# Two cross attentions in one kernel: every row block of x turned by VectorE into the moving blocks of the query products, without a DRAM copy, and in another order

## The chip, the cores and the metric

The kernel runs on one core of a Trainium2 chip. The metric is the time of one execution in microseconds, as the device reports it; the median of the runs shown is taken. All data are float32.

## What is computed

x is 4 sequences of 1024 tokens by 1024 features (4096 rows), the context 4 times 64 rows of 1024 features. Two cross attentions follow each other, and each attends from the rows of x to the 64 context rows of its own sequence:

```
# layer 0: 32 query heads of 32 features, 8 key/value heads, additive mask
q = x @ Wq + bq ; k = ctx @ Wk + bk ; v = ctx @ Wv + bv
p = softmax(q k^T / sqrt(32) + mask0)
x1 = layernorm((p v) @ Wo + bo + x) * gamma + beta
# layer 1: 16 heads of 64 features, boolean mask over the context, gated residual
a = layernorm(ctx) ; Q = x1 @ Wq1.T ; K = a @ Wk1.T ; V = a @ Wv1.T
p = softmax(where(mask1, Q K^T * 64**-0.5, -inf))
y = x1 + tanh(gate) * (p V) @ Wo1.T
```

## The kernel before, in words

**Stages.** The program has four stages. (1) Keys and values of both layers are computed from the context (to about 82 us in the profile). (2) The queries of layer 0 are computed in four blocks of 1024 tokens, numbered 0 to 3; beside block b + 1's products runs the attention of block b, one subtile of 128 tokens after the other (32 subtiles; to about 640 us). (3) Beside the attention of block 3 the key side of layer 1's query weight is folded (`folded_queries`, L729); I call this the fold stage (to about 757 us). (4) Out-projection, normalisation and layer 1 in pairs of subtiles (`project`, L394). Stage 4's code is not touched.

**A query block.** The product of the weight with a block of 1024 tokens is split in two by two blocks of 512 and done with seven products instead of eight, a Strassen-Winograd form. The stationary blocks of the weight (A11, A12, A22 and the sums S1 to S4, `left_weight`, L150) are made once. The moving blocks are made for each query block: B11, B21, B12 and B22 are quarters of the turned rows (feature half, token half), and four sums on VectorE (`right_sums`, L167 to L172) give T1 = B12 - B11 (in B12's buffer), T2 = B22 - T1, T3 = T2 - B11 and N4 = B21 - T2. So seven moving blocks are alive: B11, B21, T1, B22, T3, T2, N4. They share one pool of seven buffers (`wpool`, tag `wb`), and the next block's B11 takes the buffer of the old B11, and so on: a new moving block can be written only when the last product that reads the old one is done.

**Products.** `query_steps` (L537) lists 28 steps for a block: for i = 0 to 3 the products p1, p6, p7, p5, p3, p4, p2, each of four matmuls of 128x128 by 128x512 (L543). p1, p6, p5 and p3 add up in one bank X, p7 and p4 in V, p2 alone in W. After p1, p6, p5 and p3 ScalarE copies X out with the bias (`keep`, L551: e, z, u, f); VectorE adds (`add`, L557) V to u after p5 and to z after p4, and W to e after p2. Each finished tile is stored to `qTd` in DRAM by SP's queue (`put`, L554). Products and their operands: p1 A11 B11, p2 A12 B21, p3 S4 B22, p4 A22 N4, p5 S1 T1, p6 S2 T2, p7 S3 T3.

**Turning rows.** 256 rows ("pair") of x come in as one tile xq (`pair_rows`, four transfers of 256 KB). `turn_quarters` (L367, L370) is a 32x32 block transpose on VectorE, 128x1024 elements an instruction, two for each pair. In blocks 0 and 1 the turns write the moving blocks directly (`fill` in `rows0`, L489). In blocks 2 and 3, `store_turned` (L528) turns the rows during block 0's products into a staging tile (`stpool`) and stores it to `xTd` in DRAM; `load` (L499) brings the quarters back later as transfers of 1 MB. Rows are loaded in the order block 0, blocks 2 and 3, block 1. The moving blocks of block b + 1 are filled in block b's list of steps, after step 21 (B11), 24 (B12), 25 (B22 and three sums) and 27 (B21 and N4).

**Attention of layer 0.** `mix` (L656) does one subtile t: `front` loads q (L600) and makes the scores (matmul L611 into `big`, a pool with one buffer; VectorE L616 adds the mask), then the row maximum (L447), the subtraction (L455), the exponential on ScalarE (L456), the row sum (L465, with a reciprocal) and the division (L470). For subtile t - 1, `flip` turns the probabilities on TensorE (L640) and copies them out on ScalarE (L641), and `values` multiplies by v (L646). Between these pieces `mix` places three or four steps of the next query block, or in the fold stage the steps of `folded_queries` (matmuls L743, evictions L750).

**Order.** Each engine executes its instructions in order. The order on an engine is set when the program is built: a scheduler starts from the program order, and moves instructions where pools and dependencies let it. SP's queue carries nearly all transfers, also in order: an issue that waits for its data holds back those behind it.

Of the kernel before, what the change touches and what calls it, by code (L numbers as in the profile page):

```python
# [66 lines left out]
def tile_two_cross_attentions(  # L67
# [47 lines left out]

    x1 = [dram.tile([2 * P, H], F32, tag=f"x1_{t}", name=f"x1_{t}") for t in range(NPAIR)]
    p1 = [dram.tile([2 * P, H], F32, tag=f"p1_{t}", name=f"p1_{t}") for t in range(NPAIR)]
    xTd = {t: dram.tile([P, KC, TB], F32, tag=f"xT_{t}", name=f"xTd_{t}") for t in range(2, NBLK)}
    oTd = [dram.tile([P, KC, 2 * P], F32, tag=f"oT_{t}", name=f"oTd_{t}") for t in range(NPAIR)]
    qTd = [dram.tile([P, KC, TB], F32, tag=f"qT_{t}", name=f"qTd_{t}") for t in range(NBLK)]  # L120
    v0d = dram.tile([B * S, 256], F32, tag="v0d", name="v0d")
# [5 lines left out]
    def open_pool(stack, name, bufs, side="left"):  # L127
        return stack.enter_context(tc.tile_pool(name=name, bufs=bufs, side=side, reuse_waits="tile"))
# [3 lines left out]
    def new_block(tag, name):  # L132
        return wpool.tile([P, HK, HW], F32, tag=tag, name=name)
# [16 lines left out]
    def left_weight(w, tag, name):  # L150

        r = {"A11": block_of(w, 0, 0, tag, f"{name}_A11", True)}
        r["S2"] = new_block(tag, f"{name}_S2")
        r["S3"] = block_of(w, 0, 1, tag, f"{name}_A21", True)
        r["S1"] = new_block(tag, f"{name}_S1")
        r["S4"] = new_block(tag, f"{name}_S4")
        r["A22"] = block_of(w, 1, 1, tag, f"{name}_A22", True)
        r["A12"] = block_of(w, 1, 0, tag, f"{name}_A12", True)
        tt = nc.vector.tensor_tensor
        return r, [  # L160
            lambda: tt(r["S1"], r["S3"], r["A22"], ALU.add),
            lambda: tt(r["S3"], r["A11"], r["S3"], ALU.subtract),
            lambda: tt(r["S2"], r["S1"], r["A11"], ALU.subtract),
            lambda: tt(r["S4"], r["A12"], r["S2"], ALU.subtract),
        ]
# [21 lines left out]
    def run(steps):  # L187
        for s in steps:
            s()
# [1 line left out]

    attention = ExitStack()
    kv0pool = open_pool(attention, "kv0", 1, "right")
    rows_cm = ExitStack()
    xpool = open_pool(rows_cm, "xrows", 4, "right")
    stpool = open_pool(rows_cm, "xturned", 3, "right")
    scratch_cm = ExitStack()
    scratch = open_pool(scratch_cm, "scratch", 1)

# [6 lines left out]
    for w, n in ((wk0, "wk0"), (wv0, "wv0")):  # L206
        t = wpool.tile([P, KC, 256], F32, tag="wb", name=n)
        nc.sync.dma_start(out=t, in_=w.rearrange("(k p) o -> p k o", p=P))
        wkv0.append(t)
    def constant(ap, shape, name, dt=F32, pool=const):  # L210
        t = pool.tile(shape, dt, tag=name, name=name)
        nc.sync.dma_start(out=t, in_=ap)
        return t
# [16 lines left out]
        for a in range(NQ):  # L230
            queue.dma_start(out=t[a * Q : (a + 1) * Q], in_=v[a])

    def pair_rows(blk, i):
        xq = xpool.tile([P, 2 * NQ, QW], F32, tag="x", name=f"xq{blk}_{i}")
        at = blk * TB + i * 2 * P
        load_quarters(xq, x[at : at + 2 * P, :])
        return xq

    later = [(blk, i) for blk in xTd for i in range(4)]
    order = [(0, i) for i in range(4)] + later + [(1, i) for i in range(4)]  # L240
    ahead = []

    def more_rows():
        if order:
            ahead.append(pair_rows(*order.pop(0)))

    for _ in range(4):
        more_rows()

    ident = const.tile([P, P], F32, tag="ident", name="ident")  # L250
    make_identity(nc, ident)
# [77 lines left out]
    for e in range(2):  # L329
        for i in range(2):  # L330
            j = 2 * i + e
            for c in range(2):
# [3 lines left out]
                    in_=v0d[:, at : at + 32].rearrange("(b s) d -> s b d", b=B),  # L336
                )
    ct = transpose_ctx(1)
    for w, dst, n in ((w1k, kTd, "k1"), (w1v, vTd, "v1")):
        kvT = stpool.tile([P, KC, B * S], F32, tag="st", name=n)  # L340
        for c in range(KC):
            ps = one() if c % 2 else wx()
            for k in range(KC):
                nc.tensor.matmul(
                    ps[:, 0:256], w[k // HK, c // HK][:, k % HK, sub_ap(c % HK)], ct[:, k, :],
                    start=(k == 0), stop=(k == KC - 1),
                )
            nc.scalar.copy(kvT[:, c, :], ps[:, 0:256])
        nc.sync.dma_start(out=dst, in_=kvT)
    tanh_gate = const.tile([P, 1], F32, tag="tanh", name="tanh_gate")  # L350
    nc.scalar.activation(tanh_gate, gate_sb, AF.Tanh)
    run(w_q_sums)
# [131 lines left out]


    queries_cm = ExitStack()
    etmp = open_pool(queries_cm, "etmp", 2)

    def rows0(blk):  # L489

        r = {
            n: new_block("wb", f"x{n}_{blk}") for n in ("B11", "B21", "T1", "B22", "T3", "T2", "N4")
        }

        taken = []

        def load(n):
            h, u = {"B11": (0, 0), "T1": (0, 1), "B22": (1, 1), "B21": (1, 0)}[n]
            nc.sync.dma_start(  # L499
                out=r[n], in_=xTd[blk][:, h * HK : (h + 1) * HK, u * HT : (u + 1) * HT]  # L500
            )

        def fill(n):
            h, u = {"B11": (0, 0), "T1": (0, 1), "B22": (1, 1), "B21": (1, 0)}[n]
            for i in range(2):
                if len(taken) <= 2 * u + i:
                    taken.append(ahead.pop(0))
                turn_quarters(
                    taken[2 * u + i], r[n][:, :, i * 2 * P : (i + 1) * 2 * P],
                    (h * HK, (h + 1) * HK),  # L510
                )
                if h:
                    more_rows()

        f = load if blk in xTd else fill
        sums = right_sums(r)

        def b22():
            f("B22")
            run(sums[:3])  # L520

        def b21():
            f("B21")
            sums[3]()

        return r, {21: lambda: f("B11"), 24: lambda: f("T1"), 25: b22, 27: b21}

    def store_turned(blk, i):  # L528

        xq = ahead.pop(0)  # L530
        st = stpool.tile([P, KC, 2 * P], F32, tag="st", name=f"st{blk}_{i}")
        for h in range(2):
            turn_quarters(xq, st[:, h * HK : (h + 1) * HK, :], (h * HK, (h + 1) * HK))
        more_rows()
        nc.sync.dma_start(out=xTd[blk][:, :, i * 2 * P : (i + 1) * 2 * P], in_=st)

    def query_steps(blk, rows):  # L537

# [50 lines left out]
            keep("f", tmp["X"], i, 0)  # L589
            put("f", i, 0, 1)  # L590

        return [lambda i=i, p=p: p(i) for i in range(HK) for p in (p1, p6, p7, p5, p3, p4, p2)]

    probs = {}

# [88 lines left out]

    rows, fills = rows0(0)
    run(fills.values())
    steps = query_steps(0, rows)
    rows, fills = rows0(1)
    for n, step in enumerate(steps):
        step()  # L690
        if n % 5 in (0, 3) and later:
            store_turned(*later.pop(0))
        if n in fills:
            fills[n]()
    rows_cm.close()

    qpool = open_pool(attention, "q0", 2, "right")
    spool = open_pool(attention, "scores", 4, "right")
    ppool = open_pool(attention, "probsT", 3, "right")
# [29 lines left out]
    def folded_queries(kT, wch, k):  # L729
# [7 lines left out]
        def heads(cc):  # L737
# [8 lines left out]
                    )  # L746
            at = st[cc // 2].rearrange("p b (c e s) -> p c e b s", e=2, s=S)
            for e in range(2):
                for c2 in range(2):
                    nc.scalar.activation(  # L750
                        at[:, (cc % 2) * 2 + c2, e],
                        banks[e][:, c2 * 256 : (c2 + 1) * 256].rearrange("p (b s) -> p b s", b=B),
                        AF.Copy, scale=SCALE1,
                    )
            if cc % 2:
                n = cc // 2
                nc.sync.dma_start(
# [314 lines left out]
```

## Time and profile before

| what | value |
| --- | --- |
| three runs, us | 1986.14, 1985.75, 1980.96 |
| median, us | 1985.75 |
| the profiled execution's own time, us | 1985.84 |
| its span, us | 1983.9 |
| mean granted clock of TensorE | 0.993 of full speed |
| TensorE busy, us of the span | 1930.2 |
| VectorE busy, us of the span | 1275.6 |
| ScalarE busy, us of the span | 352.7 |
| DMA, MB moved | 317.95 |

The profile is one execution. Its engines are called PE (TensorE matmuls), PEld (TensorE weight loads), DVE (VectorE), ACT (ScalarE), POOL (GpSimd) and SP (SyncE); busy times are sums over the span, and an L number is a line of the kernel. A mark such as "<-DVE xT L172" names what ended a wait; "x8" at the end of a timeline row counts matmuls and weight loads joined in that row. PEclk is the clock that the chip granted TensorE, with 1.00 for full speed. "The slices" are the span cut in 40 equal parts, about 49.6 us each, with the busy tenths of each engine.

### The profile page before, as it was taken

The numbers are of one execution on the slowest core, as the hardware profiler recorded it, in microseconds if no ns is written. First come the engines' busy times: TensorE is split into PE (matmuls) and PEld (weight loads), VectorE is DVE, ScalarE is ACT, GpSimd is POOL, SyncE is SP. The second block draws the span as 40 slices with busy tenths as digits, with TensorE's granted clock in tenths as the row PEclk, the third lists the DMA queues.
The fourth block names the chain that finished last, engine by engine and source line by source line (L and its number), as shares of the span: only waits on it lengthen the run. The fifth ranks groups of instructions, "written<-read, shape, count | busy, mean of one in ns | idle before, by whom it ended". The sixth has DMA issues, their size and how long they took to land.

```text
span 1983.9 us, 16593 instructions
## 1 busy us (share of the span) xinstructions
PE 1930.2 (97%) x6208; PEld 921.1 (46%) x6208; DVE 1275.6 (64%) x1540; ACT 352.7 (18%) x628; POOL 236.9 (12%) x103
## 2 busy tenths in 40 slices
PE   8998999999999789999999999999999999999999
PEld 7643454554555554444443444444444444444443
DVE  3534877777777794535557667657675766576653
ACT  1101333333334684122100000000000000000000
POOL 0000000000000001445545543000000000000000
PEclk9999999999999999999999999999999999999999
DMA  8998234334335979376574335446655574647421
GB/s 279 207 245 260 66 98 156 92 98 155 93 98 180 301 255 317 118 231 203 181 223 148 116 106 138 138 124 166 165 139 147 150 180 117 168 129 180 117 85 43
DMA packets 217104, 317.95 MB, mean 160 GB/s; under 512 B 19392, under 2 KB 142656, under 8 KB 214464
## 3 DMA queue, kind: packets, MB, share of 16 engines
q1 hardware_dynamic: 197760, 287.53, 50.5%
q10 hardware_dynamic: 19264, 29.37, 5.5%
q8 instruction: 49, 0.80, 0.2%
q14 instruction: 31, 0.25, 0.0%
HBM read 190.76 MB, written 126.09 MB: 160 GB/s over the span
## 4 chain that ended last, share of the span: by engine, by line
PE 86%; DVE 7%; DMA 4%; ACT 1%; issue 1%; SPq 0%; DVEq 0%; ACTq 0%
PE wx L394 58%; PE wx L543 17%; PE big L611 3%; PE one L646 2%; PE one L640 2%; PE one L772 1%; DVE mx L447 1%; DMA xq<-in_x_dram 1%; DMA wq_A<-in_wq_dram 1%; DVE s L616 1%; DMA q<-qTd 1%; DVE s L455 1%; PE big L772 1%; DVE sm L465 1%; ACT a L750 1%
## 5 line engine op out<-in xcount | busy, mean ns | idle before, releaser
L402 DVE TENSOR_TENSOR r<-wx,r 128x512 f32<-128x512 f32 x224 | 153.7, 686 | 271.2 <-PE wx L394 267.4
L456 ACT ACTIVATE s<-s 128x1024 f32<-128x1024 f32 x96 | 101.3, 1056 | 701.0 <-DVE s L455 692.5
L797 POOL TENSOR_TENSOR r<-r,bo 128x1024 f32<-128x1024 f32 x32 | 78.1, 2448 | 840.0 <-DMA r<-in_x_dram 827.5
L465 DVE TENSOR_REDUCE sm<-s 128x16 f32<-128x1024 f32 x96 | 115.4, 1212 | 34.7 <-ACT s L456 34.7
L543 PE MATMUL wx<-xT,wq_S 128*128 128x512 f32 x256 | 123.6, 625 | 11.5 <-DVE xT L172 10.7
L406 DVE TENSOR_TENSOR s<-wx,key_bias 128x512 f32<-128x512 f32 x64 | 44.1, 689 | 137.3 <-PE wx L394 134.5
L455 DVE TENSOR_TENSOR s<-s,mx 128x1024 f32<-128x1024 f32 x96 | 118.1, 1230 | 1.4
L394 PE MATMUL wx<-wo_B,S 128*128 128x512 f32 x256 | 117.0, 599 | 0.7 <-DVE r L402 0.7
L543 PE MATMUL wx<-xB,wq_A 128*128 128x512 f32 x256 | 116.4, 597 | 0.0
L447 DVE TENSOR_REDUCE mx<-s 128x16 f32<-128x1024 f32 x96 | 115.5, 1204 | 1.3
L394 PE MATMUL wx<-b_B,pT 128*128 128x512 f32 x256 | 116.1, 593 | 0.0
L394 PE MATMUL wx<-b_B,S_p 128*128 128x512 f32 x256 | 116.0, 596 | 0.0
L616 DVE SCALAR_TENSOR_TENSOR s<-big,m 128x1024 f32<-128x1024 f32 x64 | 78.0, 1218 | 59.0 <-PE big L611 59.0
L394 PE MATMUL wx<-a_B,xT 128*128 128x512 f32 x256 | 115.4, 592 | 0.0
L394 PE MATMUL wx<-a_B,S_x 128*128 128x512 f32 x256 | 115.3, 593 | 0.0
L394 PE MATMUL wx<-wo_B,o 128*128 128x512 f32 x256 | 113.8, 595 | 0.0
L470 DVE TENSOR_TENSOR s<-s,sm 128x1024 f32<-128x1024 f32 x92 | 111.4, 1220 | 1.2
L838 POOL TENSOR_TENSOR r<-r,gamma 128x1024 f32<-128x1024 f32 x32 | 76.1, 2377 | 137.3 <-DVE r L275 137.3
L611 PEld LDWEIGHTS big<-kv,q 64*128 64x128 f32 x1024 | 67.4, 187 | 49.0 <-issue 30.6
L611 PE MATMUL big<-kv,q 64*128 64x128 f32 x1024 | 80.7, 285 | 7.0 <-DVE s L616 3.8
L839 POOL TENSOR_TENSOR r<-r,beta 128x1024 f32<-128x1024 f32 x32 | 81.0, 2531 | 2.4
L543 PEld LDWEIGHTS wx<-xT,wq_S 128*128 128x128 f32 x256 | 47.8, 196 | 67.9 <-issue 61.4
(153 smaller groups left out, 2709.8 us busy)
## 6 DMA issues: line engine op xcount, KB each, us to landing
xq<-in_x_dram SPq DMA_DIRECT2D x64, 256.0 KB, 10.0
q<-qTd SPq DMA_DIRECT2D x32, 512.0 KB, 4.7
oTd<-oT SPq DMA_DIRECT2D x32, 512.0 KB, 3.5
ad<-a SPq DMA_DIRECT2D x16, 1024.0 KB, 5.6
o<-oTd SPq DMA_DIRECT2D x16, 1024.0 KB, 8.9
r<-in_x_dram SPq DMA_DIRECT2D x32, 512.0 KB, 4.4
bd<-b SPq DMA_DIRECT2D x32, 512.0 KB, 6.5
x<-r SPq DMA_DIRECT2D x32, 512.0 KB, 2.9
```

What stands on the lines that cost most here:

```text
L394: nc.tensor.matmul(bank, a[s][:, k, :], w[m][:, k, :], start=first and k == 0, stop=last and k == HK - 1, skip_group_check=True,)
L402: nc.vector.tensor_tensor(at, bank, at, ALU.add)
L447: r = nc.vector.tensor_reduce(mx, s, AX.X, ALU.max)
L455: nc.vector.tensor_tensor(s, s, mx.unsqueeze(2).to_broadcast([P, 16, S]), ALU.subtract)
L456: nc.scalar.activation(s, s, AF.Exp)
L465: nc.vector.tensor_reduce(sm, s, AX.X, ALU.add)
L470: nc.vector.tensor_tensor(s, s, sm.unsqueeze(2).to_broadcast([P, 16, S]), ALU.mult)
L543: nc.tensor.matmul(bank, w_q[a][:, k, sub_ap(i)], rows[b][:, k, :], start=first and k == 0, stop=last and k == HK - 1, skip_group_check=True,)
L611: nc.tensor.matmul(ps[:, at : at + P], q[on, c * 4 + g, :], k0bd[on, b, c, :], start=True, stop=True,)
L616: nc.vector.scalar_tensor_tensor(s, ps.rearrange("p (h s) -> p h s", h=16), SCALE0, m.unsqueeze(1).to_broadcast([P, 16, S]), ALU.mult, ALU ...
L797: nc.gpsimd.tensor_tensor(ru, ru, bo_sb, ALU.add)
L839: nc.gpsimd.tensor_tensor(r[u], r[u], beta0_sb, ALU.add)
```

## The change

1. Staging goes: `xTd`, `stpool`, `store_turned` and `load` are removed. All rows come in in the order of the blocks. Blocks 0 and 1 have a pool of four row tiles (`xrows_0`), blocks 2 and 3 one of two (`xrows_1`); `more_rows` issues loads while buffers are free, and `done_with_rows` frees one after its turns.
2. The moving blocks of all four blocks are filled by turns directly, in another grouping: after step 22 B11 and B21 of the first two pairs, after 25 B12 and T1, after 26 B22 and the other three sums.
3. The products of each i run in the order p1, p2, p6, p7, p5, p3, p4.
4. In the fold stage each pair of evictions of 128x256 becomes one of 128x512.
5. `left_weight` loads A12 as the second block instead of the last; the keys and values of layer 1 have a pool of their own, and are stored after block 0's moving blocks are filled.

```diff
     x1 = [dram.tile([2 * P, H], F32, tag=f"x1_{t}", name=f"x1_{t}") for t in range(NPAIR)]
     p1 = [dram.tile([2 * P, H], F32, tag=f"p1_{t}", name=f"p1_{t}") for t in range(NPAIR)]
-    xTd = {t: dram.tile([P, KC, TB], F32, tag=f"xT_{t}", name=f"xTd_{t}") for t in range(2, NBLK)}
     oTd = [dram.tile([P, KC, 2 * P], F32, tag=f"oT_{t}", name=f"oTd_{t}") for t in range(NPAIR)]
     qTd = [dram.tile([P, KC, TB], F32, tag=f"qT_{t}", name=f"qTd_{t}") for t in range(NBLK)]
     v0d = dram.tile([B * S, 256], F32, tag="v0d", name="v0d")
...
     def left_weight(w, tag, name):
         r = {"A11": block_of(w, 0, 0, tag, f"{name}_A11", True)}
+        r["A12"] = block_of(w, 1, 0, tag, f"{name}_A12", True)
         r["S2"] = new_block(tag, f"{name}_S2")
         r["S3"] = block_of(w, 0, 1, tag, f"{name}_A21", True)
         r["S1"] = new_block(tag, f"{name}_S1")
         r["S4"] = new_block(tag, f"{name}_S4")
         r["A22"] = block_of(w, 1, 1, tag, f"{name}_A22", True)
-        r["A12"] = block_of(w, 1, 0, tag, f"{name}_A12", True)
         tt = nc.vector.tensor_tensor
         return r, [
             lambda: tt(r["S1"], r["S3"], r["A22"], ALU.add),
...
     attention = ExitStack()
     kv0pool = open_pool(attention, "kv0", 1, "right")
-    rows_cm = ExitStack()
-    xpool = open_pool(rows_cm, "xrows", 4, "right")
-    stpool = open_pool(rows_cm, "xturned", 3, "right")
+    early_cm = ExitStack()
+    xpools = [open_pool(early_cm, "xrows_0", 4, "right")]
+    kv1_cm = ExitStack()
+    kv1pool = open_pool(kv1_cm, "kv1", 2, "right")
     scratch_cm = ExitStack()
     scratch = open_pool(scratch_cm, "scratch", 1)
...
         t = wpool.tile([P, KC, 256], F32, tag="wb", name=n)
         nc.sync.dma_start(out=t, in_=w.rearrange("(k p) o -> p k o", p=P))
         wkv0.append(t)
     def constant(ap, shape, name, dt=F32, pool=const):
         t = pool.tile(shape, dt, tag=name, name=name)
         nc.sync.dma_start(out=t, in_=ap)
...
         for a in range(NQ):
             queue.dma_start(out=t[a * Q : (a + 1) * Q], in_=v[a])
-    def pair_rows(blk, i):
-        xq = xpool.tile([P, 2 * NQ, QW], F32, tag="x", name=f"xq{blk}_{i}")
-        at = blk * TB + i * 2 * P
-        load_quarters(xq, x[at : at + 2 * P, :])
-        return xq
-    later = [(blk, i) for blk in xTd for i in range(4)]
-    order = [(0, i) for i in range(4)] + later + [(1, i) for i in range(4)]
+    order = [(blk, i) for blk in range(NBLK) for i in range(4)]
     ahead = []
+    free = [4, 2]
     def more_rows():
-        if order:
-            ahead.append(pair_rows(*order.pop(0)))
-    for _ in range(4):
-        more_rows()
+        while order and free[order[0][0] > 1]:
+            blk, i = order.pop(0)
+            free[blk > 1] -= 1
+            xq = xpools[blk > 1].tile([P, 2 * NQ, QW], F32, tag="x", name=f"xq{blk}_{i}")
+            at = blk * TB + i * 2 * P
+            load_quarters(xq, x[at : at + 2 * P, :])
+            ahead.append(xq)
+    def done_with_rows(blk):
+        free[blk > 1] += 1
+        if len(xpools) > 1 or order[0][0] < 2:
+            more_rows()
+    more_rows()
     ident = const.tile([P, P], F32, tag="ident", name="ident")
     make_identity(nc, ident)
...
                     in_=v0d[:, at : at + 32].rearrange("(b s) d -> s b d", b=B),
                 )
     ct = transpose_ctx(1)
+    kv1 = []
     for w, dst, n in ((w1k, kTd, "k1"), (w1v, vTd, "v1")):
-        kvT = stpool.tile([P, KC, B * S], F32, tag="st", name=n)
+        kvT = kv1pool.tile([P, KC, B * S], F32, tag="k1", name=n)
         for c in range(KC):
             ps = one() if c % 2 else wx()
             for k in range(KC):
...
                     start=(k == 0), stop=(k == KC - 1),
                 )
             nc.scalar.copy(kvT[:, c, :], ps[:, 0:256])
-        nc.sync.dma_start(out=dst, in_=kvT)
+        kv1.append((dst, kvT))
     tanh_gate = const.tile([P, 1], F32, tag="tanh", name="tanh_gate")
     nc.scalar.activation(tanh_gate, gate_sb, AF.Tanh)
     run(w_q_sums)
...
     queries_cm = ExitStack()
+    xpools.append(open_pool(queries_cm, "xrows_1", 2))
     etmp = open_pool(queries_cm, "etmp", 2)
     def rows0(blk):
...
             n: new_block("wb", f"x{n}_{blk}") for n in ("B11", "B21", "T1", "B22", "T3", "T2", "N4")
         }
+        sums = right_sums(r)
         taken = []
-        def load(n):
-            h, u = {"B11": (0, 0), "T1": (0, 1), "B22": (1, 1), "B21": (1, 0)}[n]
-            nc.sync.dma_start(
-                out=r[n], in_=xTd[blk][:, h * HK : (h + 1) * HK, u * HT : (u + 1) * HT]
-            )
-        def fill(n):
-            h, u = {"B11": (0, 0), "T1": (0, 1), "B22": (1, 1), "B21": (1, 0)}[n]
+        def turn_into(name, xq, i, h):
+            at = slice(i % 2 * 2 * P, (i % 2 + 1) * 2 * P)
+            turn_quarters(xq, r[name][:, :, at], (h * HK, (h + 1) * HK))
+        def first_half():
             for i in range(2):
-                if len(taken) <= 2 * u + i:
-                    taken.append(ahead.pop(0))
-                turn_quarters(
-                    taken[2 * u + i], r[n][:, :, i * 2 * P : (i + 1) * 2 * P],
-                    (h * HK, (h + 1) * HK),
-                )
-                if h:
-                    more_rows()
-        f = load if blk in xTd else fill
-        sums = right_sums(r)
+                xq = ahead.pop(0)
+                turn_into("B11", xq, i, 0)
+                turn_into("B21", xq, i, 1)
+                done_with_rows(blk)
+        def b12():
+            for i in range(2, 4):
+                taken.append(ahead.pop(0))
+                turn_into("T1", taken[-1], i, 0)
+            sums[0]()
         def b22():
-            f("B22")
-            run(sums[:3])
-        def b21():
-            f("B21")
-            sums[3]()
-        return r, {21: lambda: f("B11"), 24: lambda: f("T1"), 25: b22, 27: b21}
-    def store_turned(blk, i):
-        xq = ahead.pop(0)
-        st = stpool.tile([P, KC, 2 * P], F32, tag="st", name=f"st{blk}_{i}")
-        for h in range(2):
-            turn_quarters(xq, st[:, h * HK : (h + 1) * HK, :], (h * HK, (h + 1) * HK))
-        more_rows()
-        nc.sync.dma_start(out=xTd[blk][:, :, i * 2 * P : (i + 1) * 2 * P], in_=st)
+            for i in range(2, 4):
+                turn_into("B22", taken.pop(0), i, 1)
+                done_with_rows(blk)
+            run(sums[1:])
+        return r, {22: first_half, 25: b12, 26: b22}
     def query_steps(blk, rows):
...
             keep("f", tmp["X"], i, 0)
             put("f", i, 0, 1)
-        return [lambda i=i, p=p: p(i) for i in range(HK) for p in (p1, p6, p7, p5, p3, p4, p2)]
+        return [lambda i=i, p=p: p(i) for i in range(HK) for p in (p1, p2, p6, p7, p5, p3, p4)]
     probs = {}
...
     rows, fills = rows0(0)
     run(fills.values())
+    for dst, kvT in kv1:
+        nc.sync.dma_start(out=dst, in_=kvT)
+    kv1_cm.close()
     steps = query_steps(0, rows)
     rows, fills = rows0(1)
     for n, step in enumerate(steps):
         step()
-        if n % 5 in (0, 3) and later:
-            store_turned(*later.pop(0))
         if n in fills:
             fills[n]()
-    rows_cm.close()
+    early_cm.close()
     qpool = open_pool(attention, "q0", 2, "right")
     spool = open_pool(attention, "scores", 4, "right")
     ppool = open_pool(attention, "probsT", 3, "right")
...
                     )
             at = st[cc // 2].rearrange("p b (c e s) -> p c e b s", e=2, s=S)
             for e in range(2):
-                for c2 in range(2):
-                    nc.scalar.activation(
-                        at[:, (cc % 2) * 2 + c2, e],
-                        banks[e][:, c2 * 256 : (c2 + 1) * 256].rearrange("p (b s) -> p b s", b=B),
-                        AF.Copy, scale=SCALE1,
-                    )
+                nc.scalar.activation(
+                    at[:, (cc % 2) * 2 : (cc % 2) * 2 + 2, e],
+                    banks[e].rearrange("p (c b s) -> p c b s", c=2, b=B), AF.Copy, scale=SCALE1,
+                )
             if cc % 2:
                 n = cc // 2
                 nc.sync.dma_start(
```

## The prediction

> **What bounds the kernel now.** I read the page first (span, engines, slices, chain), then TensorE's waits, then the busy time of every engine stage by stage, then the timeline around the edges of the stages.
>
> ```profile
> span 1983.9 us, 16593 instructions
> PE 1930.2 (97%) x6208; PEld 921.1 (46%) x6208; DVE 1275.6 (64%) x1540; ACT 352.7 (18%) x628; POOL 236.9 (12%) x103
> ...
> DMA  8998234334335979376574335446655574647421
> ...
> PE 86%; DVE 7%; DMA 4%; ACT 1%; issue 1%; SPq 0%; DVEq 0%; ACTq 0%
> ```
>
> TensorE is busy 97% of the span and carries 86% of the chain that ended last; the change takes no matmul away. The DMA engines, which the change relieves most, are on the chain for 4%. So only TensorE's few idle stretches can be won or lost. Its waits name them (engine and line <- releaser: sum us, count, longest):
>
> ```profile
> PE wx L543 <- DVE xT L172: 10.7, 2, 6.5
> ...
> PE big L611 <- DMA q<-qTd: 3.2, 3, 1.6
> PE wx L543 <- ACT u L551: 1.0, 2, 0.8
> PE wx L543 <- ACT z L551: 0.8, 1, 0.8
> ```
>
> About 16 us in all: two waits for the sum T2, three loads of q, and three small ones at evictions. The stages (start:end, length, then busy us of PE, PEld, DVE, ACT, POOL, then granted clock, DMA share, GB/s):
>
> ```profile
> 82.00:180.00 98.00, 92.72 (x210) 39.45 (x208) 39.91 (x35) 10.14 (x16) 0.00 (x0) 0.98 1.04 263
> 180.00:210.00 30.00, 23.05 (x62) 10.09 (x64) 20.45 (x15) 3.77 (x5) 0.00 (x0) 0.83 0.28 90
> 210.00:350.00 140.00, 138.13 (x631) 70.00 (x631) 110.76 (x111) 49.23 (x74) 0.00 (x0) 1.00 0.38 119
> 690.00:757.00 67.00, 58.00 (x467) 38.68 (x465) 62.79 (x63) 52.92 (x132) 0.00 (x0) 1.00 0.77 251
> 757.00:1984.00 1227.00, 1214.21 (x2871) 523.39 (x2868) 749.57 (x1016) 89.89 (x148) 229.71 (x94) 1.00 0.54 153
> ```
>
> Block 0's products keep the DMA engines full while VectorE is 41% busy; from block 1 on VectorE is 79% busy under a full TensorE; in the fold stage (690 to 757) VectorE is at 94% and TensorE waits. After 757 us (output projection, second layer) the order of instructions is the same before and after: all effects are a shift of the moment at which the fold stage ends.
>
> **The change part by part.** The sum is made against the profiled execution: 1985.84 us, of which 1983.9 span and 1.9 around it, 0.1 over the median 1985.75.
>
> *Staging removed.* Eight stores and eight loads of 1 MB go, 16.8 MB; no wait of TensorE in the list is for an xTd load and block 0's slices have TensorE near 100%, so this is worth 0. Sixteen turns leave block 0:
>
> ```profile
> L370 DVE STREAM_TRANSPOSE st<-xq 128x1024 f32<-128x1024 f32 x16 | 18.6, 1213 | 0.0
> ...
> L750 ACT ACTIVATE a<-wx 128x256 f32<-128x256 f32 x128 | 39.2, 401 | 10.0 <-PE wx L743 9.2 <-ACT wq1T L365 0.8
> ```
>
> They come back as eight turns of 1.21 us, 9.8 us, in block 1's stage (110.8 + 9.8 of 140 us, 86%) and eight in block 2's. VectorE still has 14% of room there on average, so the turns cost nothing by amount; what they cost by place comes below.
>
> *Start.* The S sums now wait for A22 as the last weight, and end about 4.6 us later (9.2 us of sums after A22's landing at 62.0, so 71.2); the rows land at 77.8 and 82.8 anyway, and cover it. B11 and B21 are filled first, so p1 and the new second product p2 (3.45 us each) run from 82.1 to 89.1. T2 is now behind e_0's eviction (0.69) on VectorE and ends at 92.2 instead of 89.8. TensorE then waits 3.1 us where it waited 4.20, with p2 already done, and the half-clock loss after it falls from 1.9 (5.37 against 3.45) to about 1.2. Net -1.7.
>
> *Inside block 0.* The order p1, p2, p6 puts a product of another bank between the eviction and its waiter: the three small ACT waits go, -1.2 with their ramps.
>
> *Entry into block 1.*
>
> ```profile
> 187.45 3.60 PE L543 MATMUL wx<-xB,wq_A 128*128 128x512 f32 x8
> 192.80 2.25 DVE L171 TENSOR_TENSOR xT<-xT,xB 128x2048 f32<-128x2048 f32 x1
> 195.08 2.29 DVE L172 TENSOR_TENSOR xT<-xB,xT 128x2048 f32<-128x2048 f32 x1
> 197.52 6.68 PE L543 MATMUL wx<-xT,wq_S 128*128 128x512 f32 x8 [6.47 <-DVE xT L172]
> ```
>
> Before: 6.47 idle, 3.2 cold (6.68 against 3.45), 0.6 of ramp, 10.3 in all. The rows are now there early, but each moving block is refilled in the buffer of the old one, so B22's turns still wait for the last p3. On VectorE the order there is: B22's two turns, T2, then the eviction u_3, then T3, N4. The last p4 of block 0 waits for u_3's bank, so TensorE idles 2 x 1.22 + 2.29 + 0.69 = 5.4 to 5.8 us, before p4 instead of after p2. Behind u_3 stand T3, N4 and z_3, so the first q load is about 1 us late. The row for the cold price: 4.20 idle cost 1.9, 6.47 cost 3.2; 5.6 lies between, 2.6. The Trainium skill ("TensorE: Matmul & The Clock Gate", section "Part 1: The HAM clock gate") has half the clock after one idle window of about 3.4 us until one busy window of as much: 1.7 here, less than either row; the stage's clock of 0.83 sides with the rows, so I take 2.6 (by the rule the sum is 0.9 lower). With 2 for the first mixes, which now carry 4 and 8 matmuls of products instead of 4 and 13: 10.6, so +0.3; from -10, if nothing stalls, to +2.
>
> *Block 1 to 2: the queue of SP.* Eight row loads for block 3 are now issued ahead of z_3's and e_0's stores and of q_8's load. In the new order on TensorE 54 matmuls of products, 13.5 products or 46 us of work, stand between the scores of subtiles 7 and 8; 22 did. So q_8 may be late without a stall at it. But what was pulled forward is missing later: mixes 8 to 12 carry 4, 7, 6, 5 and 8 matmuls of products instead of 6, 16, 12, 16 and 12. At 0.86 us a matmul and 6.34 us of attention a mix (2 x 1.16 + 2 x 1.04 + 1.94) TensorE has some 11.5 us a mix, VectorE 12.4 to 12.7 of attention alone: five mixes short by 0.9 to 1.2, with the adds 6 to 7 us, less 1.2 that this transition costs now: +5. The bounds: +2, if slack of VectorE lies before it, and +12, if every mix runs at the 13.17 us of the fold. Each gap is under 1 us; by the same rule (idle for a window) and by the clock of 1.00 in the fold, with its 0.81 gaps, that costs no clock.
>
> *Block 2 to 3.* No row loads are left; 25 matmuls between the scores of 15 and 16 against about as many; waits of 0.9 against 0.4: +0.5. The loads of pairs 2 and 3 (10.0 us each) are issued some 14 us ahead of their turns; were that cover gone, up to 5.
>
> *Fold stage.*
>
> ```profile
> 639.57 0.32 SPq L554 DMA_DIRECT2D qTd<-e  x1
> ...
> 642.63 0.57 SPq L600 DMA_DIRECT2D q<-qTd  x1
> ...
> 650.86 1.16 PE L611 MATMUL big<-kv,q 64*128 64x128 f32 x16 [1.58 <-DMA q<-qTd]
> ...
> 704.91 1.22 DVE L616 SCALAR_TENSOR_TENSOR s<-big,m 128x1024 f32<-128x1024 f32 x1 [0.81 <-PE big L611]
> ```
>
> The last store of q now is z's of p4; kT and bo, which stood between store and load on SP's queue, are issued at block 3's start. q_24 comes some 10.5 to 11 us after the last product instead of 13.5: -2.5, and the clock, 0.93 in 640 to 690, falls less: -0.7. Every fold mix lasts 13.17 us: 12.36 of VectorE and 0.81 of waiting for L611. Four evictions of 0.401 become two; a COPY of 128x512 takes 0.594 (L641), L777's of that size 0.694, so ScalarE's work is even. But the second pT copy now stands ahead of the exponential: -1.5 over eight mixes, from 0 to -5 (the waits entire). Together -4.7.
>
> Sum: -1.7 -1.2 +0.3 +5 +0.5 -4.7 = -1.8, so 1985.84 - 1.8 = 1984.0.
>
> **The rivals.**
>
> *Slower: the backlog is paid in full.* q_8 comes about 39 us after block 1's last product (9.5 now), because its store stands behind row loads. If the thin mixes then run at the fold's 13.17 us plus one add each (0.69), 13.9 against TensorE's 11.5, five of them cost 12 and a sixth makes 14, not 5: 1991 to 1993, and 1995 if the entry also takes its +2. It decides once these waits exceed 13 us in sum. For it: VectorE at 86% and five thin mixes. Against it: each product moved forward shortens the end of the block by its 3.45 us.
>
> *Faster: the entry into block 1 does not stall.* If turns and T2 run ahead of the last products, since the rows are there, the entry's 10.3 goes nearly whole: 1974 to 1976. With the fold's waits gone too, 1972. For it: no row load is late any more. Against it: the old B22 is read by the last p3, whose buffer the turns need.
>
> *It does nothing.* Gains and losses all lie under TensorE's 97%: 1985.8.
>
> **How the numbers follow.** About 0.3% (6 us) is what a measurement of this kernel can tell from no change. Near the sum, within 6 us of no change: 0.40, of which 0.08 for the case that does nothing. Backlog in full: 0.26. No stall at the entry, or a larger gain in the fold: 0.34. The sum lies 1.8 below no change and the unknown ends reach further on the gaining side at the entry and the fold (-10, -3.5) than on the losing (+7, +2), so faster by over 0.3% gets 0.34, within 0.40, slower by over 0.3% 0.26. The range goes from the entry without stall, 1973, to the backlog with the worse entry, 1995; the likeliest case's own is 1979 to 1990.
>
> **What would show it right or wrong.** In the new profile: a wait of TensorE of about 5.5 us for VectorE's u before the last p4 of block 0, and about 3 us for T2 at the start; no wait for ACT z or u in block 0; q_8's scores some 39 us after block 1's last p4, and small waits of scores or values on VectorE in mixes 8 to 12 summing to 6 or 7 us; VectorE at 83 to 86% from 210 to 500; fold evictions x64 of 0.55 to 0.7 us; DMA far under 1.0 in block 0; the stretch after the fold 1227 us as now. I am wrong if the entry has no stall, if the waits of mixes 8 to 12 exceed 13 us, if TensorE waits over 1 us for xq rows in block 1 or 2, or if the last stretch changes its length.

## The result, and the profile after

The changed kernel takes 1969.87 us in the median of its runs (1965.83 to 1970.75), the kernel before, in the same comparison, 1984.93 us (1980.96 to 1986.14): a ratio of 0.9924, with a 95% interval from 0.9903 to 0.9944. That is 15 us faster where 2 us were forecast, and 3 us below the low end of the range. Measured again later, beside the last experiments, it took 1968.91 us (0.9924, 0.9912 to 0.9936).

The page of the changed kernel, span, engines, the DMA slices and the chain by engine:

```profile
span 1969.0 us, 16487 instructions
PE 1929.0 (98%) x6208; PEld 922.9 (47%) x6208; DVE 1273.0 (65%) x1540; ACT 348.6 (18%) x564; POOL 237.6 (12%) x103
...
DMA  8972226234425888376483335455746574747421
...
PE 89%; DVE 8%; DMA 1%; issue 1%; ACT 1%; SPq 0%; DVEq 0%; ACTq 0%
```

TensorE does the same work (1929.0 us busy, 1930.2 before) in a span that is 14.9 us shorter. So all of the gain is idle or slow time of TensorE that is gone. The DMA engines are less busy in the slices of block 0 (third and fourth digit), and their share of the chain falls from 4% to 1%. The waits of TensorE (sum us, count, longest us):

```profile
PE wx L536 <- DVE xT L171: 3.1, 1, 3.1
PE wx L737 <- ACT wq1T L371: 2.9, 7, 1.5
PE big L604 <- DMA q<-qTd: 2.9, 1, 2.9
...
PE wx L536 <- DVE u L550: 1.0, 1, 1.0
```

One wait for T2 is left, the one at the start, with 3.1 us; the other, 6.5 us at the entry into block 1, is not there. Nor is the wait of about 5.5 us for u that the prediction had put in its place: the one wait for u is 1.0 us, and comes at the entry into block 3, at 518 us. The stages (length, then busy us of PE, PEld, DVE, ACT, POOL, granted clock, DMA share, GB/s):

```profile
180.00:195.00 15.00, 15.00 (x37) 6.58 (x35) 7.21 (x6) 1.37 (x2) 0.00 (x0) 1.00 0.31 104
180.00:210.00 30.00, 28.74 (x126) 14.39 (x125) 20.39 (x20) 6.70 (x9) 0.00 (x0) 1.00 0.31 97
315.00:430.00 115.00, 112.11 (x506) 55.56 (x508) 87.17 (x88) 40.38 (x60) 0.00 (x0) 1.00 0.44 119
...
743.00:1969.00 1226.00, 1213.08 (x2864) 522.44 (x2862) 750.17 (x1016) 88.88 (x144) 229.54 (x94) 1.00 0.54 152
```

At the entry into block 1, 180 to 195, TensorE is busy throughout at full clock. From 180 to 210 it is busy for 28.7 of 30 us; before it was 23.1, at a clock of 0.83. From 315 to 430 TensorE is idle for 2.9 us (1.2 before). The stretch after the fold is as long as it was (1226 and 1227 us).

The sum term by term, read from both profiled executions by the start of the first score addition of a subtile (L616 before, L609 after):

| term | forecast us | measured us | read from |
| --- | --- | --- | --- |
| context stage | 0 | +1.0 | first product 82.11, now 83.10 |
| T2 at the start | -1.7 | -1.2 | wait and cold clock: 4.20 + 1.77, now 3.14 + 1.60 |
| small waits in block 0 | -1.2 | -1.6 | 0.78 twice, none now |
| entry into block 1 | +0.3 | -9.4 | the rest to subtile 0: 207.91, now 196.68 |
| block 1's mixes | 0 | -0.4 | subtile 7: 323.45, now 311.81 |
| block 1 to 2 | +5 | +2.8 | subtile 15: 472.50, now 463.65 |
| block 2 to 3 | +0.5 | +1.4 | subtile 23: 620.68, now 613.23 |
| start of the fold | -3.2 | -3.7 | subtile 24: 652.07, now 640.91 |
| fold mixes | -1.5 | -3.0 | subtile 31: 744.42, now 730.22 |
| after it | 0 | -0.7 | spans 1983.9 and 1969.0 |

The cold clock is the length of the row after the wait (5.37, now 5.20) less the 3.60 us of such a row at full clock. The entry's row is what the rows above it leave of the shift of subtile 0. It alone is 9.7 of the 13 us that the forecast missed. The first row is not shown to be an effect of the change: the 32 matmuls of the first keys (L307, now L312) ran for 7.99 instead of 7.17 us in this execution, and in the other profiles with SP's queue alone the first product starts anywhere from 82.4 to 83.4, staged or not.

The timeline at the entry, VectorE and TensorE of the changed kernel (start us, us, engine, line, tiles, then the idle time before it and what ended it):

```profile
171.36 2.37 DVE L376 STREAM_TRANSPOSE xT<-xq 128x1024 f32<-128x1024 f32 x2 [0.46 <-PE wx L536]
173.77 2.29 DVE L170 TENSOR_TENSOR xT<-xT,xB 128x2048 f32<-128x2048 f32 x1
175.98 2.36 DVE L376 STREAM_TRANSPOSE xB<-xq 128x1024 f32<-128x1024 f32 x2
178.44 2.29 DVE L171 TENSOR_TENSOR xT<-xB,xT 128x2048 f32<-128x2048 f32 x1
180.65 0.68 DVE L550 TENSOR_TENSOR u<-wx,u 128x512 f32<-128x512 f32 x1
182.71 2.29 DVE L172 TENSOR_TENSOR xT<-xT,xB 128x2048 f32<-128x2048 f32 x1 [1.37 <-PE wx L536]
```
```profile
174.60 3.60 PE L536 MATMUL wx<-xT,wq_S 128*128 128x512 f32 x8
...
178.97 3.70 PE L536 MATMUL wx<-xB,wq_S 128*128 128x512 f32 x8
182.51 3.60 PE L536 MATMUL wx<-xN,wq_A 128*128 128x512 f32 x8
185.94 6.17 PE L536 MATMUL wx<-xB,wq_A 128*128 128x512 f32 x14
191.95 3.60 PE L536 MATMUL wx<-xT,wq_S 128*128 128x512 f32 x8
```

T1's two turns are done before 174.60, when p5, the last product that reads the old T1, only begins. B22's turns start at 175.98, 3 us before the last p3 of block 0, which reads the old B22, begins (178.97 to 182.67). T2 is complete at 180.7; p6 of block 1 asks for it at 191.95. The last p4 (182.51) follows p3 without a gap.

### The profile page after: what moved, and what is told of

Read it like the earlier page. It is cut to its first block, busy times and chain, and to the rows that moved or that the text cites. A ratio compares the mean times of both kernels' runs of the same rounds, so it can differ in the third digit from the quotient of the medians.

```text
span 1969.0 us, 16487 instructions
## 1 busy us (share of the span) xinstructions
PE 1929.0 (98%) x6208; PEld 922.9 (47%) x6208; DVE 1273.0 (65%) x1540; ACT 348.6 (18%) x564; POOL 237.6 (12%) x103
## 4 chain that ended last, share of the span: by engine, by line
PE 89%; DVE 8%; DMA 1%; issue 1%; ACT 1%; SPq 0%; DVEq 0%; ACTq 0%
PE wx L400 58%; PE wx L536 17%; PE big L604 2%; PE one L639 2%; PE one L633 2%; DVE s L609 1%; PE wx L350 1%; PE one L350 1%; DVE mx L453 1%; DVE s L461 1%; PE one L764 1%; DVE sm L471 1%; DVE s L476 1%; PE wx L737 1%; PE big L764 1%
## 5 line engine op out<-in xcount | busy, mean ns | idle before, releaser
L536 PE MATMUL wx<-xT,wq_S 128*128 128x512 f32 x256 | 118.9, 605 | 3.1 <-DVE xT L171 3.1
L609 DVE SCALAR_TENSOR_TENSOR s<-big,m 128x1024 f32<-128x1024 f32 x64 | 77.9, 1217 | 31.6 <-PE big L604 31.5
L634 ACT COPY pT<-one 128x512 f32<-128x512 f32 x128 | 69.3, 595 | 55.9 <-PE one L633 55.7
```

What stands on the lines that cost most here:

```text
L536: nc.tensor.matmul(bank, w_q[a][:, k, sub_ap(i)], rows[b][:, k, :], start=first and k == 0, stop=last and k == HK - 1, skip_group_check=True,)
L609: nc.vector.scalar_tensor_tensor(s, ps.rearrange("p (h s) -> p h s", h=16), SCALE0, m.unsqueeze(1).to_broadcast([P, 16, S]), ALU.mult, ALU ...
```

## The experiments

The forecast had three claims to be tested: that taking out the staging is worth nothing, that the entry would stall again for another reason, and that SP's queue costs 5 us from block 1 to 2. The first experiments undo or do one part. The code of the edits is shortened. The change's item 5 and the new pools of row tiles had no run of their own.

**Only the order of products** (the kernel before, staging kept):

```
-  for p in (p1, p6, p7, p5, p3, p4, p2)]
+  for p in (p1, p2, p6, p7, p5, p3, p4)]
-  return r, {21: B11, 24: T1, 25: b22, 27: b21}
+  return r, {22: first_half, 25: b12, 26: b22}   # loads from xTd in blocks 2, 3
```

> The kernel before, with only the new order of products (p1, p2, p6, p7, p5, p3, p4) and the new grouping of fills; blocks 2 and 3 stay staged in DRAM, and block 1's rows still come in last. Theory A (the entry into block 1 stops stalling because its rows are in SBUF long before their turns are due): the stall stays, TensorE waits 6 to 10 us for T2 there, and the time is 1982 to 1990. Theory B (it stops because p2 follows p1 and covers T2): the wait is under 2 us and the time is 1974 to 1977.

Measured: 1987.08 us against 1984.23, ratio 1.0014 (1.0006 to 1.0022). All its waits of TensorE from 100 to 220 us:

```profile
PE wx L556 <- DVE xT L172: 10.0, 1, 10.0
PE wx L556 <- ACT u L564: 0.8, 1, 0.8
```

```profile
193.61 0.69 DVE L570 TENSOR_TENSOR e<-wx,e 128x512 f32<-128x512 f32 x1 [6.23 <-DMA qTd<-f]
194.22 1.24 DVE L370 STREAM_TRANSPOSE xT<-xq 128x1024 f32<-128x1024 f32 x1
```

The new order alone makes the entry worse. There is 7 us of work, p1 and p2, ahead of p6, and T2 is still later, because on VectorE the turns now stand behind two additions, to z and to e. Theory B falls.

**Only the old order** (the changed kernel, nothing staged):

```
-  for p in (p1, p2, p6, p7, p5, p3, p4)]
+  for p in (p1, p6, p7, p5, p3, p4, p2)]
-  return r, {22: first_half, 25: b12, 26: b22}
+  return r, {23: first_half, 24: b12, 25: b22}
```

> The changed kernel with the old order of products (p1, p6, p7, p5, p3, p4, p2), fills after steps 23, 24 and 25, nothing staged. Theory A (rows early): no more than 2 us of wait at the entry into block 1; the start keeps its old wait of about 4 us and block 0 its small waits, so 1971 to 1975. Theory B (order): the wait for T2 of 5 us or more is back, 1978 to 1984.

Measured: 1970.82 us, ratio 0.9931 (0.9917 to 0.9944). All waits of TensorE from 100 to 220 us:

```profile
PE wx L536 <- DVE u L550: 0.3, 1, 0.3
PE wx L536 <- ACT u L544: 0.2, 1, 0.2
```

At the start the wait for T2 is 3.8 us instead of 3.1. Taking out the staging brings the gain at the entry without the new order. By the medians the order is worth 1 to 2 us, but the intervals overlap, so this is not shown.

**B22 in a buffer of its own** (the changed kernel, the other six blocks in six buffers):

```
+  if tag == "wb" and "B22" in name:
+      return wpool.tile([P, HK, HW], F32, tag="wb22", name=name, bufs=1)
```

> The changed kernel with a buffer of its own for every B22 (six buffers for the other blocks), so that the turns of a new B22 must wait for the last p3 of the old one, as the prediction had assumed. The prediction's step: TensorE idles 5.4 to 5.8 us before the last p4 of block 0, and with the cold clock the time is 1976 to 1979. Theory A: the turns do wait for p3, but p4, p1 and p2 (10 us of work) cover the two turns and T2 (4.7 us), so no wait over 1 us there and 1968 to 1972, beside what six buffers cost elsewhere.

Measured: 1968.44 us, ratio 0.9921 (0.9907 to 0.9934), as the changed kernel. Its timeline at the entry, VectorE, then TensorE:

```profile
180.29 0.69 DVE L553 TENSOR_TENSOR u<-wx,u 128x512 f32<-128x512 f32 x1 [2.89 <-ACT u L547]
184.05 2.37 DVE L379 STREAM_TRANSPOSE xB<-xq 128x1024 f32<-128x1024 f32 x2 [3.07 <-PE wx L539]
186.46 2.29 DVE L174 TENSOR_TENSOR xT<-xB,xT 128x2048 f32<-128x2048 f32 x1
```
```profile
183.85 3.60 PE L539 MATMUL wx<-xN,wq_A 128*128 128x512 f32 x8
187.28 6.17 PE L539 MATMUL wx<-xB,wq_A 128*128 128x512 f32 x14
193.29 1.88 PE L539 MATMUL wx<-xT,wq_S 128*128 128x512 f32 x4
```

Here the turns do wait for the last p3, as the prediction had them, and no product stalls (TensorE waits only 1.8 us for q_0): the addition to u now stands ahead of them, and T2 is done at 188.7, 4.5 us before p6. The step was wrong twice: the wait was not there, and with it the order on VectorE is another.

**Narrow evictions in the fold** (the changed kernel) and **wide evictions alone** (the kernel before). The edit as made in the second; the first takes it back:

```
-  for c2 in range(2):
-      nc.scalar.activation(at[:, ... + c2, e], banks[e][:, c2 * 256 : (c2 + 1) * 256]...)
+  nc.scalar.activation(at[:, (cc % 2) * 2 : (cc % 2) * 2 + 2, e], banks[e]...)
```

> The changed kernel with four evictions of 128x256 a step of the fold instead of two of 128x512. If the wide evictions make the fold mixes shorter (13.17 to 12.41 us from one score to the next), the mixes go back to about 13.1 us and the time is 1972.5 to 1975.5; if another thing made them shorter, 1969 to 1971.

> The kernel before, with only the evictions of the fold made wide (two of 128x512 for four of 128x256). If they alone shorten the fold mixes, the period goes from 13.17 to 12.4 us over the last four mixes, and the time falls by 3 to 4.5 us to 1980 to 1981.5. If they need the rest of the change (the earlier q_24), less than 1.5 us: 1983 to 1985.

Measured: narrow evictions in the changed kernel 1974.13 us, ratio 0.9947 (0.9935 to 0.9960) where the changed kernel has 0.9924 (the intervals just touch); wide ones alone 1979.57 us against 1984.10, ratio 0.9980 (0.9971 to 0.9989). In the second the last score additions start at 705.37, 717.78, 730.19 and 742.60, 12.41 us apart, as in the changed kernel, and 13.17 before. From subtile 24 to 31 the changed kernel takes 89.31 us, with narrow evictions 92.41; the kernel before takes 92.35, with wide ones 89.42: the evictions are the whole of the 3.0 us. The evictions of each kind (the groups by form, of the changed kernel and of the one with narrow evictions):

```profile
L743 ACT ACTIVATE a<-wx 128x512 f32<-128x512 f32 x64 | 35.3, 613 | 5.2 <-PE wx L737 5.0
```
```profile
L744 ACT ACTIVATE a<-wx 128x256 f32<-128x256 f32 x128 | 39.3, 409 | 4.8 <-PE wx L737 4.5
```

One of 613 ns does the work of two of 409, but neighbours overlap: the busy time falls from 39.3 to 35.3 us, a tenth. ScalarE's order changes as well. Its timeline before, with TensorE's row that waits, and after:

```profile
713.41 1.06 ACT L456 ACTIVATE s<-s 128x1024 f32<-128x1024 f32 x1
714.38 0.57 ACT L641 COPY pT<-one 128x512 f32<-128x512 f32 x1
...
715.00 1.08 PE L646 MATMUL one<-pT,kv 128*64 128x512 f32 x4 [0.42 <-ACT pT L641]
```
```profile
700.59 1.12 ACT L634 COPY pT<-one 128x512 f32<-128x512 f32 x2
701.53 1.13 ACT L462 ACTIVATE s<-s 128x1024 f32<-128x1024 f32 x1
```

The second half of pT stood behind the exponential, TensorE's values (L646) waited 0.42 us for it, and the next scores came 0.81 us after VectorE was free. Now both copies come first. The scores end at 705.35, and VectorE takes them at 705.40 without a pause. Both runs with wide evictions have the copies first, both with narrow ones have the exponential between, so how much comes from the place of the copy and how much from the shorter work is not separated.

**The order on VectorE by itself** (the kernel before, staging kept):

```
   r = nc.vector.tensor_tensor(tmp[name], bank, tmp[name], ALU.add)
+  if blk == 0 and i == 3 and name == "z":
+      tc.keep_in_program_order(r)    # behind the turns and sums of step 25
```

> The kernel before, staging and old orders kept, with one edit: the last addition to z of block 0 is pinned behind the turns and sums of the next block on VectorE, where it stood ahead of the turns of T1 and B22. Theory A1 (block 1's rows have landed by about 181 us, and only the order on VectorE, fixed when the program is built for rows that come in late, holds their turns back): the turns run from about 182, T2 is done at about 192, TensorE waits 1 to 2 us there instead of 6.5, and q_0 comes some 3 us later; the time falls by 4 to 9 us, 1975 to 1980. Theory A2 (the rows themselves are late): TensorE still waits 5 us or more for T2, 1983 to 1988.

Measured: 1977.28 us against 1984.10, ratio 0.9959 (0.9946 to 0.9973). VectorE's timeline in the kernel before, then with the addition pinned:

```profile
187.65 0.69 DVE L557 TENSOR_TENSOR z<-wx,z 128x512 f32<-128x512 f32 x1 [5.35 <-PE wx L543]
188.26 1.23 DVE L370 STREAM_TRANSPOSE xT<-xq 128x1024 f32<-128x1024 f32 x1
```
```profile
182.36 0.69 DVE L557 TENSOR_TENSOR u<-wx,u 128x512 f32<-128x512 f32 x1 [7.88 <-ACT u L551]
182.96 1.23 DVE L370 STREAM_TRANSPOSE xB<-xq 128x1024 f32<-128x1024 f32 x1
184.12 1.20 DVE L370 STREAM_TRANSPOSE xT<-xq 128x1024 f32<-128x1024 f32 x1
...
190.98 2.29 DVE L172 TENSOR_TENSOR xT<-xB,xT 128x2048 f32<-128x2048 f32 x1
```

T1's turn starts at 184.12 where it started at 188.26, none of the turns waits for a row, and TensorE waits for T2 no longer; it waits 0.78 for e and 1.7 for q_0, whose store is now behind the sums. So in the kernel before, the stall was not made by rows that were late at run time. It was made by the order on VectorE, fixed when the program was built, in which z's addition (waiting for p4) stood ahead of the turns. That the builder chose this order because it counted on late rows is the likely reason; no run shows it directly.

**Staging with everything else** (the order of products, wide evictions, and z and the next e pinned behind the turns):

```
+  return r, {22: first_half, 24: b12, 25: b22}      # block 1
+  if (blk, i, name) in ((0, 3, "z"), (1, 0, "e")):
+      tc.keep_in_program_order(r)
```

> Blocks 2 and 3 staged in DRAM as before, but with the new order of products, the wide evictions, B12 and B22 of block 1 turned after steps 24 and 25, and the last addition to z and the first to e pinned behind these turns on VectorE. If the change gains by the order on VectorE at the entry, by p2 beside p1 and by the wide evictions, and not by the staging itself, this reaches 1968 to 1973, within 4 us of the changed kernel. If taking out the 16.8 MB of traffic and the sixteen turns is itself worth something, it stays at 1976 or more.

Measured: 1974.78 us, ratio 0.9947 (0.9935 to 0.9959), between the two expectations and 5.9 us above the changed kernel beside it. VectorE, then TensorE, at the entry:

```profile
188.29 1.25 DVE L370 STREAM_TRANSPOSE xT<-xq 128x1024 f32<-128x1024 f32 x1 [3.78 <-DMA xq<-in_x_dram]
```
```profile
195.38 5.37 PE L556 MATMUL wx<-xT,wq_S 128*128 128x512 f32 x8 [2.07 <-DVE xT L172]
```

With the order repaired the rows themselves are the limit: the last pair is issued at 175.3 to 179.0, between two stores of staged tiles, and lands at 188.3. T2 is 2.07 us late, the clock falls (5.37 us for a row of 3.60, 1.8 lost), and p3's wait for u (0.78), one for q_0 (0.82) and one for a score (0.82) are there as well: 6.3 us, about what it lacks (by subtile 7 it is 5.5 us behind the changed kernel). So the staging holds the rows back; that by them it also sets the order on VectorE is likely. No run keeps the staging and loads block 1's rows first, so it stays open how much is the order of the loads and how much the traffic.

**Row loads from another queue, and later.** Both start from the changed kernel:

```
-  load_quarters(xq, x[at : at + 2 * P, :])
+  load_quarters(xq, x[at : at + 2 * P, :], nc.gpsimd if blk > 1 else nc.sync)
```

> The changed kernel with the row loads of blocks 2 and 3 issued from GpSimd's queue instead of SP's. Theory (SP's queue: the row loads for block 3 stand ahead of the last stores of q, so 54 matmuls of products are ordered between the scores of subtiles 7 and 8, and the thin mixes after it cost TensorE 2.8 us): the 54 become about 23, the scores of subtile 8 come near 340 us instead of 369, and the time falls by 2 to 3.5 us to 1966 to 1968. Rival (the thin mixes only shift work, the loss is in the turns on VectorE): 1969 to 1971.

Measured: 1981.76 us, ratio 0.9988 (0.9981 to 0.9994), 12 us slower than the changed kernel. The order on TensorE became the expected one, but there is a new wait at q_8:

```profile
349.96 2.08 PE L604 MATMUL big<-kv,q 64*128 64x128 f32 x16 [7.15 <-DMA q<-qTd]
```

The rows for block 3, issued by GpSimd at 333 and 338, were in flight when z was stored and q_8 loaded: in that stretch the store took 6.2 us and the load 8.5, where a load of q has a median of 4.7 in the kernel before and the store of z took 2.4. Besides, GpSimd's queue issued block 2's first rows at 28.7 us, among the loads of the start, and TensorE waited 7.3 us for T2 there (3.1 in the changed kernel). Neither reading of the expectation holds. Issued from another queue, the row loads no longer push the scores of subtile 8 back in the order, but in flight they still hold up the store and the load of q.

```
-  done_with_rows(blk)
+  if blk == 2: free[1] += 1          # the loads follow at step 8 of the next block
+  else: done_with_rows(blk)
+  fills = {22: first_half, 25: b12, 26: b22}
+  if blk == 3: fills[8] = more_rows
```

> The changed kernel with the first row loads of block 3 put off: not issued when block 2's rows are turned but eight steps into the next block, some 30 us later, so that SP's queue and the DMA engines are free when q_8 is stored and loaded. The order on TensorE then has 28 matmuls of products between the scores of subtiles 7 and 8 instead of 54. If these row loads cost the changed kernel its 2.8 us at the transition from block 1 to 2, it gains 1 to 2.5 us, 1966.5 to 1969; if the loss is in the turns and sums on VectorE, or q_8 is now waited for (as 7.1 us when GpSimd's queue issued the rows), 1969.5 to 1974.

> The changed kernel once more, as the yardstick for the two runs beside it: 1968 to 1971.

Measured: 1967.52 us, ratio 0.9910 (0.9896 to 0.9924); the changed kernel beside it 1968.91, 0.9924 (0.9912 to 0.9936). The intervals overlap, so by the times alone the 1.4 us are not shown. In the profiles q_8's scores start at 345.08 us, not at 367.9, and subtile 15 is 10.8 us ahead of the kernel before where the changed kernel is 8.9 ahead; the waits from 315 to 430 are down to 1.7 us from 2.7.

## Why the prediction was wrong

*Entry into block 1: +0.3.* This is the step that failed; the term measured -9.4. The prediction assumed that a new moving block takes the buffer of the old one of the same name, and so had B22's turns wait for the last p3 and TensorE idle 5.4 to 5.8 us before the last p4. The description of the kernel before says the same of the buffers. The timeline shows otherwise: the new T1 is written after p6, B22 after p7, T2 after p5 and T3 after p3. This fits buffers that are taken in the order in which they come free (the profile does not number them), and TensorE did not idle there at all. The rival "the entry does not stall" named this price (10.3 of it, 9.4 measured) and was argued down by just this assumption, with the words that the last p3 reads the buffer which the turns need. The experiment with B22's own buffer shows that it wouldn't have stalled even so.

*Staging removed: 0.* No wait of TensorE was for an xTd load, and from this the prediction put the removal at nothing. The price of staging was in the rows of block 1, which came in last, and in the order on VectorE at the entry. The prediction saw that the rows would be early, but booked it at the entry, where the assumption on the buffers took it back. The two tests with pinned additions bound it: 6.8 us is to be had with staging by order alone, and with all other edits 5.9 us still lack.

*Block 1 to 2: +5.* The sign was right, the size was not: +2.8. The scores of subtile 8 came 39.5 us after block 1's last p4, as forecast, and the mixes behind it were thin. From subtile 7 to 15, before and now:

```profile
323.45:472.50 149.05, 147.82 (x673) 75.39 (x672) 113.65 (x113) 52.70 (x80) 0.00 (x0) 1.00 0.37 115
```
```profile
311.81:463.65 151.84, 148.95 (x674) 74.26 (x673) 119.83 (x121) 53.56 (x80) 0.00 (x0) 1.00 0.42 113
```

The idle time of TensorE rose from 1.2 to 2.9 us; the other 1.1 us are busy time for the same products. The waits of the thin mixes were forecast at 6 to 7 us, and all waits of the stretch are 2.7. Standing in SP's queue does matter through the order: issued later or from another queue, the row loads let the scores of subtile 8 come at 345.1 and 350.0 us, not at 367.9. At run time q_8's load was issued at 339.5, so the order held it, not the queue. That this order costs time is seen only in a profile (1.7 of the 2.8 us with later loads), as the times do not separate the two. The rival "backlog in full", 12 to 14 us, did not come.

*Start and block 0: -1.7 and -1.2.* Near in size: -1.2 and -1.6. The wait was forecast at 3.1 and is 3.14 us; the cold loss was put at 1.2 and is 1.6 (the prediction took it against 3.45 us, the time from one product's start to the next, which makes each loss 0.15 too large). The small waits are gone, but the new order is not shown to be the reason: with the old order and nothing staged only 0.5 us of them is left, and with the new order and staging one of 0.8 stays.

*Block 2 to 3: +0.5* measured +1.4, of which 1.0 is one wait for u at the entry into block 3.

*Fold: -4.7.* Measured -6.7. The start is -3.7 against -3.2, in part by luck: q_24's scores come 9.2 us after the last product (13.5 before), more than forecast, and the clock, which was to fall less, falls more (13.6 us at half clock in the fold stage, 6.8 before). The fold mixes were mis-sized: 0.76 of the 0.81 us of waiting went on each of the last mixes (12.41 us, 13.17 before), near the far end of the stated bound, and -3.0 instead of -1.5 in all. The prediction had the copy of pT ahead of the exponential, as it came, but called ScalarE's work even, though its own figures (four of 0.401 us, two of 0.594 to 0.694) make it less; the busy time fell by a tenth.

## What to carry to other kernels

A transfer that no engine waits for can still cost time, by what it holds back and, as is likely here, by the order that is laid down when the program is built. Look at what stands ahead of a stalled chain on its engine, and ask whether its own input was there: here the rows had landed, and one addition in front of the turns cost 7 us. Before costing a wait for a buffer, read from a timeline which product really frees it; names do not tell.

## What the runs showed of the hardware that was not expected

The loss by the clock does not follow from the idle time before it. A product whose row is 3.60 us long at full clock took 5.37 after 2.07 us of idle time (staging with pins), 5.37 after 4.20 and 6.68 after 6.47 (before). After 3.14 us it took 5.20 in the changed kernel and 6.57 in the one with only the order of products: the same gap cost 1.6 us once and 3.0 another time. The granted clock at four of these places, in the order changed kernel, only the order, staging with pins, before:

```profile
92.90:96.30 3.40, 3.02 (x4) 1.50 (x5) 3.37 (x3) 0.00 (x0) 0.00 (x0) 0.51 1.14 203
```
```profile
91.60:98.30 6.70, 5.71 (x7) 2.52 (x8) 5.34 (x3) 0.00 (x0) 0.00 (x0) 0.50 1.04 202
```
```profile
196.15:199.45 3.30, 3.30 (x5) 1.35 (x4) 3.30 (x2) 0.00 (x0) 0.00 (x0) 0.50 0.03 5
```
```profile
193.40:203.50 10.10, 5.98 (x7) 2.52 (x8) 10.00 (x6) 0.00 (x0) 0.00 (x0) 0.50 0.38 105
```

Read in steps of 0.25 us, the clock stands at half for 3.4 us, 6.8, 3.4 and 10.2: one, two, one and three times 3.4. The loss comes to about half of the time that TensorE works in such a stretch. The Trainium skill ("TensorE: Matmul & The Clock Gate", section "Part 1: The HAM clock gate") tells of a free-running window of about 3.4 us with one idle window before the clock is halved. The stretches agree with the window's length; but the gap of 2.07 us, shorter than one window, was charged too, and the measurement decides.

A single gap of 0.78 us at an eviction was followed by no loss (3.70 us, against 3.60). In the fold stage of the changed kernel, where gaps of 1.49 and 0.78 us follow each other within 4 us, the clock stood at half from 652.8 to 659.6, and a score's row there took 2.08 us instead of 1.06.
